# Scores and exponentials of an attention step divided by columns of four PSUM banks instead of by banks

## The chip, the core and the metric

The kernel runs on one core of one Trainium2 chip. The metric is the device time of one execution in microseconds (us), the median of several runs. A profile is one execution recorded by the hardware profiler; its own time is given beside its span, because durations are read from that one execution.

Engines are called as the profile calls them: PE is TensorE (matmuls), PEld its weight loads, ACT is ScalarE, DVE is VectorE, POOL is GpSimd, SP is SyncE[...]. PSUM is the memory that PE writes its results to. The kernel divides it into eight banks of 512 fp32 values per partition.

## What is computed

`x` is (16, 128, 512), the context `c` is (16, 128, 128), all fp32. First comes cross attention with 32 query heads and 8 key/value heads of size 16, then a mixture of 32 experts; both are added to `x`. Cut to what matters:

```python
def _L0_xattn_ref(q, k, v):                       # k = v = ctx
    qh = q.reshape(B, S, KV, G, D).transpose(0, 2, 3, 1, 4)      # 8 KV heads x 4
    kh = k.reshape(B, S, KV, D).transpose(0, 2, 1, 3)
    vh = v.reshape(B, S, KV, D).transpose(0, 2, 1, 3)
    scores = jnp.einsum('bkgsd,bktd->bkgst', qh, kh) / scale     # scale = sqrt(16)
    weights = jax.nn.softmax(scores, axis=-1)
    out = jnp.einsum('bkgst,bktd->bkgsd', weights, vh)
    return out.transpose(0, 3, 1, 2, 4).reshape(B, S, E)
...
x = x + _L0_xattn_ref(_layernorm(x, axis=-1), ctx_512, ctx_512)
x = x + _L0_ffn_ref(_layernorm(x, axis=-1), ...)                 # router, 8 of 32 experts, shared expert
```

## The kernel before

The program has two stages. `attention_small` (L301) does the attention of all 16 batches and, woven into it, the second layer norm, the turned rows for the experts and the router's logits. `experts` follows: ranking of the tokens, the shared expert, and the routed experts. A general version of the attention (`rest`, behind a flag) is taken only if some keys are long; it is not run with these inputs.

The attention is a list of 32 steps, `items = [(b, i)]`: batch `b`, and `i` the parity of the KV head. A step handles four KV heads, `j` = 0 to 3, with their four query heads each and 128 tokens, so 512 columns per KV head.

- `scores(b, i)` (L484) issues four matmuls (L489), one per `j`. Each contracts 32 rows: the stationary operand is a 32 x 128 piece of the keys `kz` (in which `odd` has zeroed the head of the other parity), the moving operand 32 rows x 512 columns of the turned queries `qT`. `tile_position=(j * HP, 0)` puts each into its own row group of PE, so the four can run beside each other. Each result, 128 keys x 512, fills one PSUM bank. Two banks make one tile of the pool `ps_sc`, which has two such tiles, tag `sc`. In the profile every fp32 matmul stands as two records, so a step has eight.
- Two exponentials follow on ACT (L499), each over one tile of two banks, 128 x 1024, into a tile of the SBUF pool `pp` (five of them).
- `values(b, i)` (L502) multiplies the exponentials with the values `va` (four matmuls, L505, 512 columns each, weights of 32 columns, one column group per `j`), and DVE copies the result (L514). A column of ones in `va` gives the sums of the exponentials along.
- `transposes(...)` (L447) turns up to two sets into one PSUM tile of the pool `ps_x` (L459): queries of a batch to come (`queries`, copied out by ACT at L480), normalized rows for the router (`turn_of`, ACT, L543), and the output of `values` (`added`, divided and added by DVE and POOL, L523 to L532).

The order of the instructions on PE, ACT, DVE and POOL is written out by hand; each engine works its queue in that order. In the loop over `n` (L650), PE gets per step: scores of step n, values of step n-1, in some steps the gate's matmuls (`gate_parts`, L566, and `gate_sums`, L581), then the transposes: one set in step 1 and in the odd steps up to 11 (none in step 0), two sets in most others. `head`, `middle` and `tail` hang further work of DVE, POOL and ACT on the steps; what of it is ACT's: `keys` (L373, ahead of the scores of steps 4, 5, 9, 11, 17 and 19) and `squares` (L394, steps 21, 23, 25 and 27). Waits between engines are put in by the framework from the tiles that instructions read and write.

Behind the last step the two tiles of `ps_sc` are used again: `two` (L685) for transposes, and `gu` (L686), two banks, for the first matmuls of the shared expert (`filler`, L282).

Of the kernel before, what the change touches and what calls it, by code (L numbers as in the profile page):

```python
# [9 lines left out]
F32 = mybir.dt.float32  # L10
F16 = mybir.dt.float16
I32 = mybir.dt.int32
AF = mybir.ActivationFunctionType
ALU = mybir.AluOpType
AX = mybir.AxisListType
PSUM = bass.MemoryType.PSUM
DRAM = bass.MemoryType.DRAM

P = 128
EPS = 1e-5  # L20
HD = 16
# [25 lines left out]
def tile_xattn_moe(  # L47
# [15 lines left out]
    nc = tc.nc  # L63
    B, S, D = x.shape
    E, _, ND, I = w1.shape
# [4 lines left out]
    TB = 512  # L70
# [93 lines left out]
    rows = dram.tile([NT * P, D + E], F32, name="rows")  # L164
# [66 lines left out]
    def gate_rows(b, eng):  # L231
        xn = xnp.tile([P, D], F32, tag="xn2", name="xn2", bufs=4)
        normalized(xn, xs[b], b, SECOND, eng)
        nc.sync.dma_start(rows[ts(b, P), 0:D], xn)
        xn2[b] = xn
# [61 lines left out]
    HP = 2 * HD  # L297
    NJ = KV // 2
    quarter = [slice(4 * k, 4 * k + 4) for k in range(NTB)]

    def attention_small():  # L301


        with ExitStack() as ph:
            kpool = ph.enter_context(tc.tile_pool(name="kp", bufs=1))
            ap2 = ph.enter_context(tc.tile_pool(name="ap2", bufs=2))
            pp = ph.enter_context(tc.tile_pool(name="pp", bufs=5))
            ps_sc = ph.enter_context(tc.tile_pool(name="ps_sc", bufs=2, space=PSUM))
            ps_x = ph.enter_context(tc.tile_pool(name="ps_x", bufs=1, space=PSUM))
            ps_lg = ph.enter_context(tc.tile_pool(name="ps_lg", bufs=1, space=PSUM))  # L310
            ps_oT = ph.enter_context(tc.tile_pool(name="ps_oT", bufs=1, space=PSUM))
            qTs, ps, oTs, xqs = {}, {}, {}, {}
            cn = kpool.tile([P, B, KV * HD], F32, name="cn")
            cTs = kpool.tile([P, B, P], F32, name="cTs")

# [53 lines left out]
            kzs = [kpool.tile([P, 4, 2, P], F32, name=f"kz{k}") for k in range(2)]  # L369
# [69 lines left out]
            H = P // 2  # L439
            halves = [slice(h * H, (h + 1) * H) for h in range(2)]  # L440

            def bank_pair(pool):
                return pool.tile(
                    [P, 2, 2, 2, P], F32, tag=("x" if pool is ps_x else "sc"), name="x"
                )

            def transposes(*sets, x=None, between=()):  # L447

                x = bank_pair(ps_x) if x is None else x
                for s, (of, split, _) in enumerate(sets):  # L450
                    for k in range(4):
                        for h, rows in enumerate(halves):
                            if split:
                                to = x[:, h, :, s, ts(k, P // 4)]
                                by = ident[rows, rows].rearrange("p (a b) -> p a b", a=2)
                            else:
                                to = x[:, h, k // 2, s, ts(k % 2, H)]
                                by = ident[rows, rows]
                            nc.tensor.matmul(  # L459
                                to,  # L460
                                lhsT=of[rows, k, :],
                                rhs=by,
                                start=True,
                                stop=True,
                                is_transpose=True,
                                tile_position=(h * H, 0),
                            )
                for s, (_, _, then) in enumerate(sets):
                    if s == len(sets) - 1:
                        for f, a in between:  # L470
                            f(*a)
                    then(x[:, :, :, s])
# [9 lines left out]
                return xn, False, then  # L482

            def scores(b, i):  # L484
                scs = [ps_sc.tile([P, 2, TB], F32, tag="sc", name="sc") for _ in range(NJ // 2)]
                qT = qTs[b].rearrange("p h r s -> p (h r s)")
                for j in range(NJ):
                    rows = slice(j * HP, (j + 1) * HP)
                    nc.tensor.matmul(  # L489
                        scs[j // 2][:, j % 2],  # L490
                        lhsT=kzs[b // 4 % 2][rows, b % 4, i, :],
                        rhs=qT[rows],
                        start=True,
                        stop=True,
                        tile_position=(j * HP, 0),
                    )
                for j, sc in enumerate(scs):
                    p = pp.tile([P, 2, TB], F32, tag="p", name="p")
                    nc.scalar.activation(p, sc, AF.Exp, scale=1.0 / HD**0.5)  # L499
                    ps[b, i, 2 * j], ps[b, i, 2 * j + 1] = p[:, 0], p[:, 1]  # L500

            def values(b, i):  # L502
                oT = ps_oT.tile([P, TB], F32, tag="oT", name="oT")
# [37 lines left out]
            def turn_of(b, copy=nc.scalar.copy):  # L541
                def then(x):
                    copy(  # L543
                        xnT[b // 4][:, :, ts(b % 4, P)].rearrange(
                            "p (r k) (h s) -> p h r k s", r=2, h=2
                        ),
                        x.rearrange("p h r (k s) -> p h r k s", k=2),
                    )

                return xn2.pop(b).rearrange("p (k d) -> p k d", d=P), False, then  # L550
# [95 lines left out]
            parts[31] = 8  # L646

            transposes(queries(0))
            keep_warm(FILL[-1])
            for n in range(N):  # L650
                for f, a in head.get(n, ()):
                    f(*a)

                scores(*items[n])
                if n == 1:
                    transposes(queries(1))
                if n > 0:
                    values(*items[n - 1])
                if n in parts and n < N - 1:
                    gate_parts(parts[n])  # L660
                sets = []
                if n % 2 == 0 and 0 < n // 2 < B - 1:
                    sets.append(queries(n // 2 + 1))
                if n in turned:
                    sets.append(turn_of(turned[n]))
                if n > 1:
                    sets.append(added(*items[n - 2], nc.gpsimd if n < N - 1 else nc.vector))
                if n == N - 1:
                    sets.reverse()
                between = middle.get(n, ())  # L670
                if sets:
                    transposes(*sets, between=between)
                else:
                    assert not between
                keep_warm(FILL.get(n, 0))
                if n in sums:
                    gate_sums(sums[n])
                for f, a in tail.get(n, ()):
                    f(*a)
# [2 lines left out]

            gate_rows(12, nc.gpsimd)
            nc.scalar.activation(table, table, AF.Sigmoid)
            two = bank_pair(ps_sc)  # L685
            gu = ps_sc.tile([P, 2, TB], F32, tag="sc", name="gu")  # L686
            banks = iter([gu[:, i] for i in range(2)])
            later, products = [], []
            matmuls = shared_up(0, 0, lambda: next(banks), later, products)

# [20 lines left out]
            filler(1)  # L711
            gate_parts(12)
            gate_rows(15, nc.vector)
            transposes(turn_of(15), x=bank_pair(ps_sc))
            gate_rows(14, nc.vector)
            transposes(turn_of(14, nc.vector.tensor_copy))
            gate_sums(12, nc.scalar.copy)
# [1199 lines left out]

    pieces = [(k, i) for k in range(NTB) for i in range(NI)]
    left_over = attention_small()
    experts(pieces[1:], in_order, *left_over)  # L1920
    left = nc.values_load(
# [64 lines left out]
```

## Time and profile before

| what | value |
|---|---|
| median of 3 runs | 876.24 us (875.76 to 877.6) |
| profiled execution: its time / its span | 875.97 us / 874.1 us |
| granted PE clock, mean | 0.997 |
| exponentials L499, ACT, 128 x 1024 | 64, 62.1 us busy, mean 1023 ns |
| score matmuls L489, PE, 512 columns | 256 records, 44.2 us busy |
| value matmuls L505, PE, 512 columns | 256 records, median 605 ns |
| ACT waiting for scores (L499 <- PE sc L489) | 13.2 us in 22 waits |
| score weight loads waiting for exponentials (PEld sc L489 <- ACT p L499) | 4.7 us in 13 waits, within 8.80 to 106.00 |
| scores of step 0 start / last step's start | 8.83 / 102.76 us |
| last matmul of the program ends | 864.66 us |

Times inside the profile are counted from the span's start. "Busy" is the union of an engine's instruction records; matmuls overlap in it, so a row group's matmuls that run beside each other count once. A name such as `p<-sc` is the tile written and the tile read. A releaser behind an arrow (`<-ACT p`) is what an engine's idle time ended with. The chain of waits is the sequence of pieces, each released by the one before it, that leads to the end of the span or of a window; its shares say which work the time went through.

### The profile page before, as it was taken

The page shows a single profiled execution, that of the slowest core. Times are in us where ns is not written, and L with a number is a line of the kernel's source. Part 1 is how long each engine was busy: PE and PEld are TensorE (multiplying, and loading weights), DVE is VectorE, ACT ScalarE, POOL GpSimd, SP SyncE. Part 2 cuts the span into 40 slices and gives each one's busy share as a digit, 9 for nine tenths or more (in the row PEclk, how much of TensorE's full clock was granted, in tenths as well). Part 3 has the DMA queues.
Part 4 walks back from the last instruction along what each step waited for, and adds up shares of the span by engine and source line. Part 5 has one row for each costly group of instructions (what it writes and reads, how often), then busy time and mean ns, then how long its engine had stood idle before and what let it go on. Part 6 is the DMA issues. An engine that isn't in the chain of part 4 may idle for free.

```text
span 874.1 us, 13629 instructions
## 1 busy us (share of the span) xinstructions
PE 860.4 (98%) x4015; PEld 539.0 (62%) x4015; DVE 625.7 (72%) x1599; ACT 689.3 (79%) x1570; POOL 478.7 (55%) x590
## 2 busy tenths in 40 slices
PE   8999999999999999999999999999999999999995
PEld 5344444545665666666666666676667777777763
DVE  7877778859877777777777777786777677777410
ACT  5889732539998898879898989898798889899721
POOL 4487560044355666566556665655555555664554
PEclk9999999999999999999999999999999999999998
DMA  9111112657567787788778777877787677776654
GB/s 301 66 49 40 60 50 70 218 152 206 154 176 158 171 192 200 165 174 192 159 178 195 204 171 186 197 199 177 169 180 183 166 168 195 180 188 166 94 79 53
DMA packets 59877, 137.15 MB, mean 157 GB/s; under 512 B 12169, under 2 KB 16393, under 8 KB 59793
## 3 DMA queue, kind: packets, MB, share of 16 engines
q0 software_dynamic: 32032, 69.25, 41.0%
q1 hardware_dynamic: 27680, 66.81, 22.8%
q8 instruction: 34, 0.56, 0.3%
q14 instruction: 51, 0.41, 0.2%
q10 hardware_dynamic: 80, 0.13, 0.1%
HBM read 96.71 MB, written 46.73 MB: 164 GB/s over the span
## 4 chain that ended last, share of the span: by engine, by line
PE 92%; POOL 3%; issue 2%; DMA 2%; ACT 1%; DVE 0%; POOLq 0%; ACTq 0%
PE p L1611 43%; PE y L1749 24%; PE gu L282 6%; PE sc L489 5%; PE oT L505 4%; PE y L1386 3%; PE x L459 2%; POOL out_dram L1721 2%; DMA out_dram<-yw,token 2%; PE gu L1541 2%; PE tok L1038 1%; PE lgT L566 0%; PE lg L581 0%; ACT p L499 0%; PE rank L1277 0%
## 5 line engine op out<-in xcount | busy, mean ns | idle before, releaser
L1506 ACT COPY xall<-blocks 32x256 f32<-32x256 f32 (+10 forms) x1137 | 419.1, 369 | 15.0
L1721 POOL DMA_INDIRECT out_dram<-yw,token x150 | 243.6, 1624 | 210.7 <-DMA out_dram<-yw,token 78.6
L1749 PE MATMUL y<-wdn,sa 128*128 128x512 f32 (+2 forms) x672 | 259.1, 594 | 0.0
L1460 POOL DMA_INDIRECT xgs<-rows,token x138 | 155.4, 1126 | 128.1 <-DVE token L1050 53.2
L1611 PE MATMUL p<-xall,wup 128*128 128x270 f32 (+27 forms) x720 | 185.4, 394 | 0.0
L1611 PEld LDWEIGHTS p<-xall,wup 128*128 128x128 f32 x720 | 136.7, 190 | 44.1 <-issue 16.9
L1749 PEld LDWEIGHTS y<-wdn,sa 128*128 128x128 f32 (+2 forms) x672 | 100.9, 171 | 83.7 <-issue 70.5
L1765 ACT ACTIVATE yw<-y,wt 128x512 f32<-128x512 f32 x138 | 94.7, 686 | 71.0 <-PE y L1749 39.0
L1611 PE MATMUL p<-t,s 128*128 128x270 f32 (+27 forms) x480 | 125.6, 394 | 0.0
L1611 PEld LDWEIGHTS p<-t,s 128*128 128x128 f32 x480 | 91.1, 190 | 37.6 <-issue 22.4
L1509 DVE STREAM_TRANSPOSE blocks<-xgs 128x512 f32<-128x512 f32 x138 | 97.3, 705 | 0.2
L1621 DVE TENSOR_TENSOR z<-u,p 128x270 f32<-128x270 f32 (+27 forms) x96 | 48.8, 508 | 66.9 <-PE p L1611 63.2
L499 ACT ACTIVATE p<-sc 128x1024 f32<-128x1024 f32 x64 | 62.1, 1023 | 13.3 <-PE sc L489 13.2
L1611 PE MATMUL p<-t,wup 128*128 128x270 f32 (+27 forms) x240 | 63.7, 396 | 0.0
L1611 PE MATMUL p<-xall,s 128*128 128x270 f32 (+27 forms) x240 | 63.5, 395 | 0.0
L1611 PEld LDWEIGHTS p<-t,wup 128*128 128x128 f32 x240 | 45.1, 190 | 24.8 <-issue 14.1
L282 PE MATMUL gu<-xall,sup 128*128 128x512 f32 x128 | 59.2, 602 | 0.0
L1621 DVE TENSOR_TENSOR u<-u,p 128x270 f32<-128x270 f32 (+27 forms) x48 | 24.4, 508 | 44.2 <-PE p L1611 37.1
L1611 PEld LDWEIGHTS p<-xall,s 128*128 128x128 f32 x240 | 45.3, 190 | 15.9 <-issue 3.9
L1506 DVE COPY xall<-blocks 32x256 f32<-32x256 f32 (+11 forms) x187 | 50.7, 298 | 3.5
L489 PE MATMUL sc<-qT,kz 32*128 32x512 f32 x256 | 44.2, 639 | 0.5 <-ACT p L499 0.2
L1602 DVE TENSOR_TENSOR t<-xall,t 128x540 f32<-128x540 f32 (+27 forms) x60 | 43.4, 723 | 0.5
(218 smaller groups left out, 916.0 us busy)
## 6 DMA issues: line engine op xcount, KB each, us to landing
wup<-in_w_dram SPq DMA_DIRECT2D x64, 512.0 KB, 4.8
wdn<-in_w_dram SPq DMA_DIRECT2D x32, 512.0 KB, 5.9
rows<-xn SPq DMA_DIRECT2D x16, 256.0 KB, 2.0
out_dram<-x SPq DMA_DIRECT2D x16, 256.0 KB, 3.3
x<-in_x_dram SPq DMA_DIRECT2D x15, 256.0 KB, 5.3
out_dram<-yw,token POOLq DMA_INDIRECT x150
xgs<-rows,token POOLq DMA_INDIRECT x138
cTs<-in_cT_dram SPq DMA_DIRECT2D x4, 256.0 KB, 4.7
```

The source lines that it names most:

```text
L282: nc.tensor.matmul(acc, lhsT=sup[:, w, d, ts(i, P)], rhs=xnT[k][:, d, :], start=(d == 0), stop=(d == ND - 1),)
L489: nc.tensor.matmul(scs[j // 2][:, j % 2], lhsT=kzs[b // 4 % 2][rows, b % 4, i, :], rhs=qT[rows], start=True, stop=True, tile_position=(j * ...
L499: nc.scalar.activation(p, sc, AF.Exp, scale=1.0 / HD**0.5)
L1460: nc.gpsimd.indirect_dma_start(out=t, out_offset=None, in_=rows[:, :], in_offset=bass.IndirectOffsetOnAxis(ap=token[:, j : j + 1], axis=0) ...
L1506: yield on_ACT, 1 + many, lambda dst=dst, of=of, copy=copy: copy(dst, of)
L1509: nc.vector.transpose(blocks[:, j % NB_BUF, :], xgs[:, j % NG_BUF, 0:D])
L1602: yield lambda o=out_, a=a, b=b: nc.vector.tensor_tensor(o, a, b, ALU.subtract)
L1611: nc.tensor.matmul(acc[:, i, 0:h], lhsT=w[:, i, d, :], rhs=x[:, d, :], start=(first and i == d == 0), stop=(i == outs[-1] and d == 1), ski ...
L1621: soon(lambda: nc.vector.tensor_tensor(out_, a, b, ALU.add))
L1721: ins = nc.gpsimd.indirect_dma_start(out=flat, out_offset=bass.IndirectOffsetOnAxis(ap=token2[:, k - 1 : k] if a else token[0:b, j : j + 1 ...
L1749: nc.tensor.matmul(y[c0:c1, :], lhsT=acts_of[k % NA][:, i, col : col + c1 - c0], rhs=wdn[k % NW][:, i, :], start=(i == 0), stop=(i == NI - 1),
L1765: nc.scalar.activation(yws[j], y, AF.Copy, scale=wt[:, j : j + 1])
```

## The change

`ps_sc` now holds one tile `sc` for the whole attention, `[P, NJ, 2, TB // 2]`: four banks (index `j`), each split into two halves of 256 columns (index `h`). A step issues, for `h` = 0 and then 1, four matmuls of 256 columns, one into each bank, followed by one exponential over that half of all four banks (128 x 4 x 256, the same 1024 columns). There are eight score matmuls a step in place of four, with half the columns; the number of exponentials and their size stay. The exponentials of a step go to one tile `p` of four times 512 columns; `pp` has three such tiles (before, five tiles of half the size). `values` reads the same columns as before. The scratch `two` is now banks 0 and 1 of `sc`, the banks of `gu` are its banks 2 and 3.

```diff
-            pp = ph.enter_context(tc.tile_pool(name="pp", bufs=5))
-            ps_sc = ph.enter_context(tc.tile_pool(name="ps_sc", bufs=2, space=PSUM))
+            pp = ph.enter_context(tc.tile_pool(name="pp", bufs=3))
+            ps_sc = ph.enter_context(tc.tile_pool(name="ps_sc", bufs=1, space=PSUM))
...
+            sc = ps_sc.tile([P, NJ, 2, TB // 2], F32, name="sc")
...
             def scores(b, i):
-                scs = [ps_sc.tile([P, 2, TB], F32, tag="sc", name="sc") for _ in range(NJ // 2)]
-                qT = qTs[b].rearrange("p h r s -> p (h r s)")
+                p = pp.tile([P, NJ, 2, TB // 2], F32, tag="p", name="p")
+                qT = qTs[b].rearrange("p h r s -> p h (r s)")
+                for h in range(2):
+                    for j in range(NJ):
+                        rows = slice(j * HP, (j + 1) * HP)
+                        nc.tensor.matmul(
+                            sc[:, j, h],
+                            lhsT=kzs[b // 4 % 2][rows, b % 4, i, :],
+                            rhs=qT[rows, h],
+                            start=True,
+                            stop=True,
+                            tile_position=(j * HP, 0),
+                        )
+                    nc.scalar.activation(p[:, :, h], sc[:, :, h], AF.Exp, scale=1.0 / HD**0.5)
                 for j in range(NJ):
-                    rows = slice(j * HP, (j + 1) * HP)
-                    nc.tensor.matmul(
-                        scs[j // 2][:, j % 2],
-                        lhsT=kzs[b // 4 % 2][rows, b % 4, i, :],
-                        rhs=qT[rows],
-                        start=True,
-                        stop=True,
-                        tile_position=(j * HP, 0),
-                    )
-                for j, sc in enumerate(scs):
-                    p = pp.tile([P, 2, TB], F32, tag="p", name="p")
-                    nc.scalar.activation(p, sc, AF.Exp, scale=1.0 / HD**0.5)
-                    ps[b, i, 2 * j], ps[b, i, 2 * j + 1] = p[:, 0], p[:, 1]
+                    ps[b, i, j] = p[:, j].rearrange("p h t -> p (h t)")
...
-            two = bank_pair(ps_sc)
-            gu = ps_sc.tile([P, 2, TB], F32, tag="sc", name="gu")
-            banks = iter([gu[:, i] for i in range(2)])
+            two = sc[:, 0:2].rearrange("p h r (s t) -> p h r s t", s=2)
+            banks = iter([sc[:, i].rearrange("p h t -> p (h t)") for i in (2, 3)])
...
-            transposes(turn_of(15), x=bank_pair(ps_sc))
+            transposes(turn_of(15), x=two)
```

The helper `bank_pair` is gone; `transposes` takes its tile from `ps_x` itself when it is given none.

## The prediction, made before the changed kernel ran

> **What bounds the kernel now.** I read the page's first rows, then the table by windows, to see which engine fills the attention stage, 8.80 to 106.00 us, and what follows it.
>
> ```profile
> PE 860.4 (98%) x4015; PEld 539.0 (62%) x4015; DVE 625.7 (72%) x1599; ACT 689.3 (79%) x1570; POOL 478.7 (55%) x590
> ```
>
> ```profile
> 8.80:106.00 97.20, 96.77 (x1008) 39.75 (x1009) 76.49 (x187) 81.59 (x103) 57.66 (x115) 1.00 0.27 93
> 106.00:146.00 40.00, 38.46 (x228) 18.46 (x228) 30.48 (x117) 10.80 (x21) 15.91 (x154) 1.00 0.09 34
> 146.00:868.00 722.00, 718.66 (x2740) 474.60 (x2738) 513.54 (x1278) 594.10 (x1442) 398.97 (x288) 1.00 0.73 173
> ```
>
> The columns after the window's length are busy PE, PEld, DVE, ACT and POOL. TensorE (PE) is the bound everywhere: behind the attention it stands idle 1.5 us of 40 and 3.3 us of 722, so time lost in the attention goes into the end time almost whole. Within the attention, PE's 96.77 us is not all streaming, so I read the chain of waits of that window: its line shares, then one pair of steps.
>
> ```profile
> by line: PE sc L489 43.4%; PE oT L505 30.7%; PE x L459 19.1%; PE lg L581 2.3%; ACT p L499 2.1%; PE lgT L566 1.8%; PE gu L282 0.6%; issue 0.3%; PE kT L411 0.2%
> ...
> 40.98 1.07 PE sc L489 x8
> 42.05 1.00 PE oT L505 x8
> 43.05 0.39 PE x L459 x8
> 43.44 1.82 PE sc L489 x8
> 45.26 1.00 PE oT L505 x8
> 46.26 0.64 PE x L459 x16
> ```
>
> A step is scores, values of the step before, transposes. The scores take 1.07 when nothing stops them and up to 1.82 when their second pair of banks is still being read by the last step's second exponential. In all they hold 43.4% of 97.2 = 42.2 us, 1.32 a step; without any wait 32 x 1.07 = 34.2. So about 8 us of the stage is waiting for ScalarE: all that a better overlap could win. The timeline of ScalarE and PE shows the couplings that I need.
>
> ```profile
> 42.15 1.94 ACT L499 ACTIVATE p<-sc 128x1024 f32<-128x1024 f32 x2
> 44.60 1.94 ACT L499 ACTIVATE p<-sc 128x1024 f32<-128x1024 f32 x2 [0.52 <-PE sc L489]
> ...
> 48.07 1.94 ACT L499 ACTIVATE p<-sc 128x1024 f32<-128x1024 f32 x2 [0.54 <-PE sc L489]
> ```
>
> ```profile
> 43.37 1.90 PE L489 MATMUL sc<-qT,kz 32*128 32x512 f32 x8
> ...
> 46.83 1.14 PE L489 MATMUL sc<-qT,kz 32*128 32x512 f32 x8
> ```
>
> Unhindered scores start at 46.83, the last ends 1.14 later (47.97), and the exponentials start at 48.07: 0.10 from PE to ScalarE. In the step at 43.37 the second pair ends at 45.27, so it began at 44.13, 0.04 to 0.05 after the exponential that ended at 44.09: that is the release back to PE. One exponential takes 1.02 (the page: x64, mean 1023 ns).
>
> **The change, part by part.** *The waits.* The first group of four matmuls now fills columns 0 to 255 of all four banks, the first exponential reads those, the second group fills the other halves. [...] Row first: in the step at 43.37 the second pair streams from 44.13 to 45.27 while the first exponential reads from 44.60 on; they are in different banks. [...] By columns, as the change has it, the second group could stream under the first exponential[...]. No trace of before has two engines in one bank, but the order of the built program decides it: the second group of each step waits for that step's first exponential, and the first group of the next step for the second exponential. (The transposes of the odd steps have lost their own wait for ScalarE, as the new one covers it.) So scores and exponentials of a step run one after the other: group, exponential, group, exponential. Behind the waiting second group PE's queue holds the values of the step before and the transposes, which have nothing to do with that exponential.
>
> *The group.* Four matmuls of 512 columns take 1.07 to the next start. Half is 0.54. The row nearest to four matmuls of 256 columns is the gate's.
>
> ```profile
> 82.93 0.61 PE L566 MATMUL lgT<-xall,gw 128*32 128x256 f32 x8
> ```
>
> It loads 32 weight columns, not 128 (weight loads: 110 ns against 182). [...] The eight records of a group are two passes over the same row groups[...]. The rows alone, 0.61 with its tail, put it at 0.55 to 0.62; I take 0.64, as it explains the 0.08 that score passes are longer than value passes (records start 0.53 against 0.45 apart). The last result comes 0.07 after the next start (1.14 - 1.07), so a group is complete at 0.71.
>
> *The exponential.* Same 1024 columns, now four runs of 256, strided on both sides. The query copy reads runs of 128 (512 in 586 ns), the gate copy a plain run (256 in 378): 0.81 ns a column, as the exponential has from 512 to 1024 ((1023 - 586)/512 = 0.85). Runs cost nothing that shows; bounds 0 and 5% (+3 us in all), I take 0.
>
> *One step.* Scores start at 0; complete 0.71; exponential from 0.81 to 1.83; second group from 1.88; values at 1.88 + 0.64 = 2.52, where before it was 1.32. The second exponential ends at 1.88 + 0.71 + 0.10 + 1.02 = 3.71, and PE comes to the next scores at 2.52 + 1.00 + 0.39 = 3.91 at the earliest (one set of transposes) or 4.16 (two): the wait across steps is gone, by 0.15 to 0.4. Sum for steps 1 to 31: 31 x 2.52 = 78.1, against 42.2 - 1.1 (step 0) = 41.1: **+37.0**.
>
> *Step 0.* Its first exponential starts at 10.00 as before (ScalarE copies values until then), ends 11.02; second group 11.07; second exponential 11.88 to 12.90; step 1 starts at 12.95, before at 11.07: **+1.9**.
>
> *ScalarE's queue.* The first exponential is now waited for by PE at once, so what ScalarE does before it counts.
>
> ```profile
> 23.26 0.58 ACT L480 COPY qT<-x 128x512 f32<-128x512 f32 x1
> 23.74 0.73 ACT L373 ACTIVATE kz<-cTs,odd 128x512 f32<-128x512 f32 x1
> 24.39 1.94 ACT L499 ACTIVATE p<-sc 128x1024 f32<-128x1024 f32 x2
> ```
>
> That step's scores start at 23.15, so copy and keys hold the exponential until 1.24 after the start in place of 0.81. A copy alone ends in time (0.11 + 0.49 = 0.60). Keys come behind a copy in steps 5, 9, 11, 17 and 19: 5 x 0.43 = 2.1; squares in steps 21, 23, 25, 27 (85.29 - 84.12 = 1.17): 4 x 0.36 = 1.4. **+3.5**, 1.5 to 5.5. Two small waits of PE for ScalarE outside the scores (steps 4 and 9) go: **-0.3**.
>
> *At nothing:* fewer, larger `p` buffers (3 steps in place of 2.5), since values follow one step behind; VectorE and GpSimd, whose work stays the same and had 20 and 40 us to spare; the two score pairs used as scratch behind step 31, where the order is the same and the banks are free by then (3.71 against 4.16). If work behind the attention had waited for something else than PE, it could give back at most the 1.5 us idle there; I take 0.
>
> Sum: 37.0 + 1.9 + 3.5 - 0.3 = +42.1. The profiled execution took 875.97 (span 874.1 and 1.9 around it), so 918.1; it lies 0.27 below the median of 876.24, which gives **918.3**.
>
> **Rivals.** *Faster: the columns do run free.* If the second group streams under the first exponential, PE pays 2 x 0.64 = 1.28 a step and waits for nothing, as the exponential starts 0.4 earlier: 31 x 1.28 = 39.7 against 41.1, 874.8; with a hidden reload 31 x 1.07, 868.3. It decides from the point where the second group's wait is met before PE gets there; ScalarE's 2.4 a step would fit under PE's 2.7. Middle 872. For it: 8 us of waits are there to win. Against it: the wait in the built program[...]. 2%.
>
> *Much slower: the clock falls.* PE now stands 1.25 of some 4 us in every step. If that takes the granted clock to half, 2.9 us of streaming a step double: +90, 1008. Against it, the windows behind the last matmul (864.66):
>
> ```profile
> 864.70:868.50 3.80, 0.00 (x0) 0.00 (x0) 0.00 (x0) 0.69 (x1) 2.57 (x2) 1.00 0.81 115
> 868.60:872.00 3.40, 0.00 (x0) 0.00 (x0) 0.00 (x0) 0.00 (x0) 0.00 (x0) 0.50 0.04 9
> ```
>
> The clock held 1.00 for 3.8 us without a matmul; the new gaps are a third of that. 3%.
>
> **How the numbers follow.** The serial case has 95%. Its low end: groups at the gate's row (0.10 sooner and 0.09 shorter: -5.9), queue -2, 1.5 given back: 909. Its high end: exponential +3, queue +2, both weight loads dearer (182 - 110 ns each, +0.05 twice a step: +3): 927. The rivals' 5% stay outside the range. A change within 0.2% is about what measurement cannot tell here; nothing lands there but the dearest form of the first rival: faster 2%, same 1%, slower 97%.
>
> **What would show it.** In the profile after: the score line at some 80 us of the attention's chain together with exponentials, PE idle some 1.2 us in nearly every step "<-ACT p" ahead of the second four matmuls, no two exponentials back to back (they stand in pairs of 1.94 now), 32 steps in about 139 us, granted clock 1.00, and everything behind shifted unchanged. It is wrong if exponentials overlap the second group's records, if score groups take 0.54, or if the stage behind takes more or less than its 762 us.

## The result, and the profile after

The changed kernel takes 925.0 us, the median of six runs (920.72 to 930.74). The kernel before takes 876.04 us in its six runs beside it (875.76 to 877.6). The ratio is 1.056, interval 1.052 to 1.060: slower, by 49 us. The forecast was 918.3, with a range of 909 to 927.

The profiled execution is the slowest of the six, 930.74 us (span 928.9). Its page, first the engines' row and the clock's, then the two costly groups that the change touches:

```profile
PE 873.0 (94%) x4271; PEld 548.3 (59%) x4271; DVE 626.3 (67%) x1599; ACT 694.5 (75%) x1570; POOL 479.4 (52%) x590
...
PEclk7989999999999999999999999999999999999998
...
L495 ACT ACTIVATE p<-sc 128x1024 f32<-128x1024 f32 x64 | 65.5, 1023 | 45.3 <-PE sc L487 44.0
...
L487 PE MATMUL sc<-qT,kz 32*128 32x256 f32 x512 | 49.7, 460 | 42.0 <-ACT p L495 41.7
```

ScalarE has the same 64 exponentials at the same mean of 1023 ns, but now stands idle 44.0 us for score matmuls (13.2 before); PE stands idle 41.7 us for exponentials (0.2 in the same row before). Each engine waits for the other. And a row that was expected to stay as it was did not: the mean granted clock is 0.982, and the dip is in the first slices, where the attention is.

The table by windows, cut at the same points of the program as before (attention; 40 us behind it; the routed experts):

```profile
8.80:159.80 151.00, 109.15 (x1263) 49.06 (x1263) 76.65 (x187) 86.53 (x103) 57.76 (x119) 0.91 0.18 62
159.80:199.80 40.00, 38.14 (x232) 18.45 (x229) 29.69 (x116) 10.81 (x21) 15.30 (x150) 1.00 0.09 31
199.80:921.80 722.00, 719.35 (x2741) 474.86 (x2739) 514.79 (x1279) 594.34 (x1442) 400.21 (x288) 1.00 0.74 173
```

All of it is in the first window: from the first score to the first matmul of the shared expert it is 150.9 us, before 96.9. From there to the last matmul it is 759.3 us, before 758.9. DVE and ACT have the same number of instructions in the attention as before (187 and 103; POOL has 119 in this window and had 115); PE has 255 records more, at a granted clock of 0.91.

The chain of waits over the attention, by lines, and a step on PE and on ScalarE from the timeline (start, length, engine, line, and in brackets the idle time before it with what ended it):

```profile
by line: PE sc L487 27.5%; PE oT L502 23.8%; ACT p L495 21.6%; PE x L456 13.3%; issue 4.5%; DMA cn<-in_c_dram 4.0%; ACT qT L477 2.4%; PE lg L578 1.5%; ACT sq L395 1.3%; PE lgT L563 1.1%; PE warm L354 1.0%; ACT kz L374 0.6%; ACT va L383 0.4%
```

```profile
41.44 0.71 PE L487 MATMUL sc<-qT,kz 32*128 32x256 f32 x8
43.36 0.71 PE L487 MATMUL sc<-qT,kz 32*128 32x256 f32 x8 [1.20 <-ACT p L495]
44.00 1.06 PE L502 MATMUL oT<-p,va 128*32 128x512 f32 x8
```

```profile
42.28 1.02 ACT L495 ACTIVATE p<-sc 128x1024 f32<-128x1024 f32 x1
44.14 1.02 ACT L495 ACTIVATE p<-sc 128x1024 f32<-128x1024 f32 x1 [0.83 <-PE sc L487]
```

First group 41.44, complete 42.15; exponential 42.28 to 43.30; second group 43.36; values 44.00. The exponentials stood in pairs before; now each has a group of matmuls ahead of it and, for the first, one behind it that waits. From scores to values it is 2.56 us at full clock, where before it was 1.32 on average. The exponential, 2.1% of the chain before, is 21.6% of it.

The clock in two windows in a row (length, then busy time and instructions of PE, PEld, DVE, ACT and POOL, then the granted clock):

```profile
48.88:52.29 3.41, 1.84 (x36) 1.20 (x32) 3.06 (x7) 2.36 (x4) 0.49 (x1) 1.00 0.02 5
52.29:55.71 3.42, 3.42 (x28) 1.22 (x24) 1.24 (x4) 1.02 (x1) 0.23 (x1) 0.50 0.00 0
```

PE worked 1.84 of 3.41 us at the full clock; the next 3.41 us were granted half of it. The changes of the clock in this trace lie 3.41 us or a multiple of it apart (11.33, 21.57, 52.29, 55.71). Eight windows of 3.41 us at half clock, 27.3 us, lie in the attention of this execution, three of them before 21.6 us. The steps in them are longer than other steps of their kind by 10.9 us in all (0.25 to 2.1 each). The other five executions show mean clocks of 0.986 to 0.996 and are shorter in that order.

### The profile page after: what moved, and what is told of

The parts are those of the page before. It is cut to its first block, busy times and chain, and to the rows that moved or that the text cites. A ratio compares the mean times of both kernels' runs of the same rounds, so it can differ in the third digit from the quotient of the medians.

```text
span 928.9 us, 14113 instructions
## 1 busy us (share of the span) xinstructions
PE 873.0 (94%) x4271; PEld 548.3 (59%) x4271; DVE 626.3 (67%) x1599; ACT 694.5 (75%) x1570; POOL 479.4 (52%) x590
## 4 chain that ended last, share of the span: by engine, by line
PE 87%; ACT 5%; issue 3%; POOL 2%; DMA 2%; SPq 0%; DVE 0%; POOLq 0%; ACTq 0%; DVEq 0%
PE p L1607 41%; PE y L1745 23%; PE gu L282 5%; PE sc L487 4%; PE oT L502 4%; ACT p L495 4%; PE y L1382 3%; PE x L456 2%; POOL out_dram L1717 2%; PE gu L1537 1%; DMA out_dram<-yw,token 1%; PE tok L1034 1%; PE sc L282 1%; DMA cn<-in_c_dram 1%; PE lg L578 0%
## 5 line engine op out<-in xcount | busy, mean ns | idle before, releaser
L495 ACT ACTIVATE p<-sc 128x1024 f32<-128x1024 f32 x64 | 65.5, 1023 | 45.3 <-PE sc L487 44.0
L487 PE MATMUL sc<-qT,kz 32*128 32x256 f32 x512 | 49.7, 460 | 42.0 <-ACT p L495 41.7
L511 DVE COPY oTs<-oT 128x512 f32<-128x512 f32 x32 | 22.1, 691 | 60.0 <-PE oT L502 60.0
L529 POOL TENSOR_TENSOR x<-x,at 128x256 f32<-128x256 f32 x30 | 21.8, 725 | 72.2 <-DVE at L522 72.2
L487 PEld LDWEIGHTS sc<-qT,kz 32*128 32x128 f32 x512 | 21.7, 198 | 60.1 <-ACT p L495 55.7
```

The source lines that it names most:

```text
L487: nc.tensor.matmul(sc[:, j, h], lhsT=kzs[b // 4 % 2][rows, b % 4, i, :], rhs=qT[rows, h], start=True, stop=True, tile_position=(j * HP, 0),)
L495: nc.scalar.activation(p[:, :, h], sc[:, :, h], AF.Exp, scale=1.0 / HD**0.5)
```

## The experiments

My theory when they began had four parts. (A) PE and ScalarE work in turns because the second group waits for the first exponential, and PE's queue blocks what stands behind it; this is worth some +43. (B) The wait comes from the shared banks. (C) Part of the time is the second load of the same weights. (D) On top, the clock falls where PE stands idle. The rival to B is that the wait comes with the one lasting tile, whatever the banks; the rival to C, that the load is hidden; the rival to D, that PE's idle time drops the clock by its length alone. Kernel before beside them: 875.9 on each chip.

| label | change | median (range), us | ratio, interval |
|---|---|---|---|
| e1 | one lasting tile, divided by banks | 883.75 (883.69 to 884.01) | 1.0087, 1.0072 to 1.0101 |
| e2 | by columns, both exponentials after all matmuls | 883.97 (883.82 to 885.48) | 1.0094, 1.0079 to 1.0109 |
| e3 | the change, gap filled with full matmuls | 922.07 (920.85 to 922.34) | 1.0521, 1.0507 to 1.0534 |
| e4 | the change, gap filled with thin matmuls | 926.5 (922.81 to 927.33) | 1.0568, 1.0549 to 1.0586 |
| e5 | before, with split score matmuls | 876.15 (875.97 to 878.15) | 1.0005, 0.9997 to 1.0013 |
| e6 | the change, values moved into the gap | 903.36 (902.02 to 903.61) | 1.0303, 1.0287 to 1.0319 |
| e9 | e3, without filling in five steps | 922.35 (922.13 to 923.47) | 1.0529, 1.0514 to 1.0543 |

One further run of e4, 947.61 at a mean clock of 0.963, is left out of its row; no trace of it was kept. Three more kernels (e7, e8, e10) compute half of the heads and are read in their attention alone: their attention values differ, a general part (`rest`) ran behind, and so their totals, about 3.6 ms, say nothing.

**e1: the lasting tile without the columns.** Four matmuls of 512 columns into the four banks of the one tile, then an exponential on banks 0 and 1 and one on banks 2 and 3, as the kernel before has it with two tiles.

```diff
-                for h in range(2):
-                    for j in range(NJ):
...
-                            sc[:, j, h],
...
+                for j in range(NJ):
...
+                        sc[:, j].rearrange("p h t -> p (h t)"),
...
+                for k in (slice(0, 2), slice(2, 4)):
+                    nc.scalar.activation(p[:, k], sc[:, k], AF.Exp, scale=1.0 / HD**0.5)
```

> One lasting tile of four banks and three large p buffers, but scores and exponentials divided by banks as before. Theory 'by tile' (a score matmul waits for every earlier exponential on its tile, whichever banks that reads): the scores of a step wait for the second exponential of the step before, so a step lasts at least 1.14 + 0.12 + 1.94 + 0.05 = 3.25 us where it was 2.71 or 3.2 in turns: 29 steps, 94.3 against 88.3, about 882. Theory 'by bank' (only a shared bank makes it wait): the tile changes nothing, 876.

It measured 883.75, 7.9 above before. Its timeline, first the exponentials of one step on ScalarE, then the scores of the next two steps on PE:

```profile
35.89 1.94 ACT L495 ACTIVATE p<-sc 128x1024 f32<-128x1024 f32 x2 [1.32 <-PE sc L486]
```

```profile
37.88 1.14 PE L486 MATMUL sc<-qT,kz 32*128 32x512 f32 x8 [0.48 <-ACT p L495]
...
41.14 1.14 PE L486 MATMUL sc<-qT,kz 32*128 32x512 f32 x8 [0.73 <-ACT p L495]
```

All four matmuls start together at 37.88, when the second exponential of the step before has ended (35.89 + 1.94 = 37.83). The one into bank 0 has no bank in common with that exponential, which reads banks 2 and 3, and it waits all the same. So the wait comes with the tile, and B is refuted. This part of the change alone makes a step as long as its scores and both exponentials one after the other: 3.26 here, 3.03 on average before (96.9 / 32).

**e2: the columns without the turns.** The change, with the exponentials moved behind all eight matmuls.

```diff
                             tile_position=(j * HP, 0),
                         )
+                for h in range(2):
                     nc.scalar.activation(p[:, :, h], sc[:, :, h], AF.Exp, scale=1.0 / HD**0.5)
```

> All eight score matmuls of a step first, then the two exponentials, still by columns. The wait inside the step is gone, the wait across steps and the second weight load stay. Serial theory: a step lasts 1.28 + 0.07 + 0.12 + 1.94 + 0.05 = 3.46, about 889.5; the wait inside a step is then worth some 30 of the 44 us. If the loss were in the 256-column matmuls or in the strided exponentials, it would stay at 915 to 920. PE is used more, so the clock should hold 1.00.

It measured 883.97, the same as e1, 5.5 under the expectation, at mean clocks of 0.996 and 0.997 (0.995 to 0.998 before). On PE:

```profile
37.90 1.15 PE L487 MATMUL sc<-qT,kz 32*128 32x256 f32 x16 [0.48 <-ACT p L496]
38.98 1.06 PE L503 MATMUL oT<-p,va 128*32 128x512 f32 x8
```

Eight matmuls of 256 columns hold PE for 1.08, as long as four of 512 (1.07). Loading the weights twice costs nothing, which speaks against C. Dividing by columns is harmless in itself: it is free in PE and, as the exponential keeps its 1.02 with four runs of 256, free in ScalarE. What costs is the order, an exponential between the groups of one tile: from 884.0 to 919.3, the change's time at full clock (derived under e3 and e9).

**e5: the reload alone.** The kernel before, each score matmul of 512 columns issued as two of 256, pair of banks by pair of banks.

```diff
-                for j in range(NJ):
+                for k, h, j in [(k, h, 2 * k + d) for k in range(2) for h in range(2) for d in range(2)]:
...
-                        scs[j // 2][:, j % 2],
+                        scs[k][:, j % 2, cols],
```

> The kernel before, each score matmul of 512 columns issued as two of 256 (tiles, banks and exponentials as before). If the weight load of 128 columns is paid again per group[...], scores take 1.28 in place of 1.07 where nothing stops them, less where they wait for an exponential: 879 to 882. If it hides: 876.

```profile
46.99 1.16 PE L490 MATMUL sc<-qT,kz 32*128 32x256 f32 x16
```

It measured 876.15, a ratio that is no different from 1, with scores 1.09 long where they were 1.07: C is refuted. The single records, whose starts I take from the trace of e2, show how. Its four rounds of records (one record per row group in each; in the trace of before, the four of a round start within 0.02 and last 0.69 or 0.59 each) start at 0, 0.321, 0.537 and 0.753, and the values at 1.075. Rounds in the middle are 0.216 apart, each with a load of 128 weight columns of its own. Where matmuls of the routed experts follow in a row in the trace of before, they start 0.216 apart with 256 columns (L1541) and 0.429 with twice as many (L1749): the columns account for all of it, and no load shows. Some 0.105 more is seen twice. In the first round (0.321 = 0.105 + 0.216) it fits a load that nothing covers: in the trace of before the two loads of a row group start 0.108 apart there (46.83 and 46.94). In the hand-over to the values (0.322) it does not fit one: the values load 32 columns, and their own first round, 0.453 in place of 0.429, is only 0.024 longer for it. What fills the hand-over stays open. In the kernel before it is the same: 0, 0.535 and 1.070, with 0.429 for 512 columns. Both ends are paid once per block. The second group of the changed kernel is a block by itself: its second round starts 0.320 after its first (43.36 and 43.68), and the values 0.324 after that (44.00), 0.64 in all.

**e6: other work into the gap.** The values of the step before, which need neither exponential of this step, are issued between the two groups.

```diff
-                scores(*items[n])
+                scores(*items[n], (lambda: values(*items[n - 1])) if n > 0 else None)
...
-                if n > 0:
-                    values(*items[n - 1])
```

> The changed kernel with the values of the step before issued between the two score groups. Serial theory: PE's work now fits under the exponentials, and the chain group, exponential, group, exponential sets the step: 2 x (0.71 + 0.12 + 1.02 + 0.05) = 3.8 us, about 904, with the clock at 1.00 or nearly. If PE's own time set the step, it would change nothing: 920 to 930.

It measured 903.36, as expected. On PE, a step's second group (its transposes, left out, follow), then the next step's first group, the values that were moved, and its second group:

```profile
41.13 0.71 PE L489 MATMUL sc<-qT,kz 32*128 32x256 f32 x8 [0.21 <-ACT p L497]
...
42.99 0.71 PE L489 MATMUL sc<-qT,kz 32*128 32x256 f32 x8 [0.50 <-ACT p L497]
43.63 1.07 PE L504 MATMUL oT<-p,va 128*32 128x512 f32 x8
45.00 0.71 PE L489 MATMUL sc<-qT,kz 32*128 32x256 f32 x8 [0.30 <-ACT p L497]
```

From group to group it is 1.86 and 2.01, and each waits for an exponential: groups and exponentials in turns are now the whole step (3.87 here; 3.95 or 4.20 in the changed kernel at full clock), and values and transposes lie beside them. The clock held 1.00 in the attention, but behind it one window fell to half:

```profile
143.01:146.42 3.41, 2.55 (x33) 1.91 (x34) 0.69 (x1) 1.52 (x5) 0.00 (x0) 1.00 0.00 0
146.42:149.83 3.41, 3.41 (x5) 1.35 (x5) 2.44 (x8) 2.08 (x3) 3.29 (x7) 0.50 0.01 2
```

In this execution (903.61) the part behind the attention takes 761.0 us, against 759.3 in the other changed forms, so at full clock e6 is some 901.9. Of the 43 us that the change costs at full clock, the work blocked behind the waiting group is then 919.3 - 901.9 = 17; the turns themselves are the other 26.

**e7, e8, e10: tile or bank, in the changed order.** With two KV heads in place of four, each half of the columns can have banks to itself. e7 keeps the change's layout, both halves in the same two banks of the tile; e10 puts the second half into two other banks of the same tile; e8 gives it a tile of its own.

```diff
-                    for j in range(NJ):
+                    for j in range(2):
...
e7    sc[:, j, h]              exponential from sc[:, 0:2, h]
e10   sc[:, 2 * h + j, 0]      exponential from sc[:, 2 * h : 2 * h + 2, 0]
e8    scs[h][:, j, 0]          exponential from scs[h][:, :, 0]
```

> The changed kernel with two KV heads per step in place of four in scores and exponentials (values use their weights twice, the other heads' scores are left out), both halves of the columns in the same two banks. Second group starts 0.71 + 0.12 + 0.59 + 0.05 = 1.47 after the first, values at 2.11; about 903 at full clock, more by what the clock loses, as the array is used less.

> The same with half the heads left out, but the second half of the columns in two other banks, in a tile of its own. The second group needs no exponential of its step: it starts 0.64 after the first, values at 1.28, about 874; against the one with shared banks some 28 us less for the same work. If the reload and the smaller matmuls were the cost, both would take the same.

> Half the heads left out as before; the second half of the columns goes to two other banks, but of the same tile. If the wait comes with the tile, the second group starts 1.45 after the first, as with shared banks; if it comes with the bank, 0.5 to 0.64 after it, as with two tiles.

The timelines on PE, first e7, then e10, then e8:

```profile
44.22 0.70 PE L487 MATMUL sc<-qT,kz 32*128 32x256 f32 x4
45.68 0.70 PE L487 MATMUL sc<-qT,kz 32*128 32x256 f32 x4 [0.76 <-ACT p L495]
```

```profile
43.22 0.70 PE L487 MATMUL sc<-qT,kz 32*128 32x256 f32 x4
44.68 0.70 PE L487 MATMUL sc<-qT,kz 32*128 32x256 f32 x4 [0.76 <-ACT p L495]
```

```profile
42.16 1.13 PE L487 MATMUL sc<-qT,kz 32*128 32x256 f32 x8
43.22 1.07 PE L502 MATMUL oT<-p,va 128*32 128x512 f32 x8
```

The second group starts 1.46 after the first whether it shares banks with the exponential or not; with a tile of its own it follows at once, and values start after 1.06 in place of 2.09 (1.28 was expected, with the reload that e5 rules out). That is the rival to B again, now in the order that costs the time. The clock of e7 fell as well: it was 0.50 from 50.90 to 54.31, and 0.976 to 0.983 in the mean of its four runs. A version of the whole step with a tile for each half and, as in all kernels here, a bank for each score matmul of a half needs all eight banks into which the kernel divides PSUM for its scores, and the transposes, the gate and the values hold four. It was not built, nor was a layout with two heads in one bank; no kernel here beats the one before.

**e3, e4: the clock.** Idle matmuls on zeros are put into the gap ahead of the second group, whose results nobody reads: three of 128 x 128 x 128 (e3), or four of 32 x 32 x 128 (e4). They are meant to fill PE's time about alike (in e3 the three take 0.94 at 42.10) and to differ in how much of the array they use. In both kernels the tile of the idle matmuls is taken anew at each use, from the pool that the gate uses too.

```diff
                 for h in range(2):
+                    if h == 1:
+                        keep_warm(3)       # e4: four matmuls idle[0:32] <- wz[0:32, 0:32], wz[0:32]
                     for j in range(NJ):
```

> The changed kernel with three idle matmuls of 128 x 128 x 128 on zeros in PE's gap between the two score groups; they end before the exponential does. Clock theory (the granted clock falls when the array's use in a window of 3.41 us is below some 0.37): no half-clock window in the attention, all runs within 919 to 922. Rival (the spread of 921 to 931 comes from something else, as from the DMAs): time and spread as in the changed kernel.

> As the run with full idle matmuls, but each fills 32 rows x 32 columns of the array only: the gap is busy, the array's use hardly rises (some 0.015). If use counts, the clock still falls in some windows and runs lie at 921 to 931; if the length of the gap or PE's busy time counts, no window falls and all runs are within 919 to 922.

The attention of e3 by windows, then two windows in a row of e4:

```profile
8.70:150.30 141.60, 125.49 (x1455) 68.95 (x1455) 76.67 (x187) 86.41 (x103) 58.68 (x124) 1.00 0.19 66
```

```profile
141.54:144.96 3.42, 3.06 (x44) 2.27 (x40) 2.38 (x6) 1.61 (x2) 0.72 (x1) 1.00 0.16 62
144.96:148.37 3.41, 3.41 (x33) 1.14 (x25) 0.69 (x1) 1.02 (x1) 0.00 (x0) 0.50 0.23 82
```

In the profiled run of e3 the clock stays at 1.00, and it takes 920.85, ten less than the profiled run of the change with the same serial steps; its runs spread over 1.5 us and not 10. The cure is not whole: three of the five runs, 922.07 to 922.34 and so at or just over the expected end, show a mean clock of 0.994 to 0.995 in place of 0.997. That would fit one more window at half clock; they have no trace. About 1.55 us of the 920.85 are waits that the idle matmuls add (their bank is also the gate's, and in step 31 they wait 1.3 for its reader), so the change at full clock is some 919.3. In e4 a window in which PE is 89% busy is followed by half the clock, so the thin matmuls did not hold it up; the runs of e4 lie where they were expected if use counts. D stands in the form that use decides; its rival, the length of idle time, is refuted.

To see what does count I took every window of 3.41 us in the attention of ten profiles (before, after, e1 to e8), and added up for each matmul its rows x columns of the array x columns streamed, as a share of 128 x 128 at 1.2 columns per ns (512 columns took 0.429 us above, 1.19 per ns).

| window granted | next one | windows | share of the array used | PE busy |
|---|---|---|---|---|
| full clock | half | 15 | 0.14 to 0.379 | 0.44 to 0.89 |
| full clock | full | 307 | 0.353 and up, nearly all over 0.383 | 0.54 and up |
| half clock | half | 35 | up to 0.378 | 0.67 to 1.00 |
| half clock | full | 14 | 0.386 and up | 0.94 and up |

Use of about 0.38 parts them in both directions, with an overlap of three windows; busy time does not separate them. The attentions of e9 and e10, which were not used to find the boundary, agree: six windows of 0.25 to 0.34 were followed by half the clock, six at half clock with 0.389 and more by the full one, and those that stayed at half have 0.372 at most, though two that stayed at full clock have only 0.366 and 0.369. The kernel before ran its attention at 0.55 and more. The longest gap in the windows of the changed kernel that fell was 1.7 us. What exactly the chip counts stays open: the share is a quantity that parts these windows, and of its factors only the size of the idle matmuls was varied on purpose.

**e9: fill only where it seems needed.** e3 without idle matmuls in steps 18, 22, 26, 30 and 31, to save the waits that they add there.

```diff
-                    if h == 1:
+                    if h == 1 and 2 * b + i not in (18, 22, 26, 30, 31):
```

> As the run with full idle matmuls, but without them in steps 18, 22, 26, 30 and 31, where they waited for a reader of the gate's bank and held the step up by 3.3 us in all. If serial waits and the clock are all there is, this is the changed kernel at full clock: 918 to 919, up to 1.5 more where one of the five bare steps falls into a window of low use. The prediction's sum without a clock term was 918.3.

A miss: 922.35, no better than e3. In its profile two windows with half the clock came back (106.94 to 110.35 and 144.48 to 147.90), behind windows with bare steps. The first of them, with the one ahead of it:

```profile
103.53:106.94 3.41, 2.21 (x32) 1.36 (x32) 1.70 (x5) 1.61 (x2) 1.39 (x5) 1.00 0.00 0
106.94:110.35 3.41, 3.41 (x32) 1.48 (x28) 1.15 (x2) 1.60 (x3) 2.63 (x10) 0.50 0.00 0
```

The steps in them are 2.7 longer. Step 0 is another 0.44 longer than in e3, as the context lands later there (ScalarE starts to copy it at 9.82 in place of 9.36). The profiled run took 922.49; 922.49 - 2.7 - 0.44 = 919.35, the same full-clock time as from e3.

## Why the prediction was right, and where its reasons were not

**The serial step: right.** 2.52 was forecast from scores to values, 2.56 measured; over 31 steps that is 1.2 more than the sum had. At full clock the change costs 919.3 - 875.9 = 43.4, against a sum of 42.1.

**ScalarE's queue: right, a little smaller.** Steps with keys behind a copy are +0.37 (0.43 forecast), steps with squares +0.27 (0.36): 5 x 0.37 + 4 x 0.27 = 2.9 in place of 3.5. Step 14 is +0.32, which the forecast did not have; its cause stays open.

**At nothing: right.** Exponentials over runs of 256 keep 1023 ns; what lies behind the attention is 0.4 longer; the wait across steps is gone in most steps, as the step is now longer than that wait.

**Why the second group waits: the wait was read rightly from the built program, its reason wrongly.** I put it down to the banks that the second group shares with the exponential: an assumption, which no trace of before shows. What two engines in one bank at once would do, no kernel here shows either. The wait is the framework's, for the tile: e1 and e10 have it with separate banks, e8 is free of it with separate tiles. It made no difference to the time, but it would have to the cure: other banks of the same tile do not help.

**The group of 0.64: right number, wrong working.** It was my estimate, and that a load is paid in each of a group's two passes was not shown by any trace of before. With 0.108 for a load of 128 columns, as the loads at 46.83 and 46.94 stand apart, it is (1.07 - 2 x 0.108)/2 + 2 x 0.108 = 0.64. e5 and e2 refute the working for these matmuls: the same reload inside a running block costs nothing (ratio 1.0005). Of the two loads that the estimate counted, one is real, at the start of a block (0.321 in place of 0.216 in e2); the other 0.105 stands at the hand-over to the values, where no load of that size is due. With two passes in a group both accounts give 0.64, which is luck. With four they part, and there the wrong one made the expectation for e2 5.5 too high.

**The clock: the step that failed.** It was a rival at 3%, written as all or nothing: +90 if the clock falls, nothing otherwise, and dismissed because it had held 1.00 for 3.8 us without a matmul. That view does not show how much idle time a window of 3.41 us may hold. The clock fell in part, in 8 windows of the profiled execution. The windows of 3.41 us do not keep step with the kernel's 3.95 or 4.20, so it is likely that in each execution others of them hold too little work; the other five runs have a mean clock and no trace. Against 919.3 the fastest run is 1.4 us longer, the profiled one 11.4 (10.9 read from its steps, the other 0.5 at its two ends), the median 5.7. These 5.7 are what is left over, not a measurement of their own, and the clock is their only cause that the traces show: 875.9 + 43.4 + 5.7 = 925.0. The range of 909 to 927 held the median without a term for this cause, so that part of the hit is luck; two of the six runs, 927.79 and 930.74, lie beyond its end. The length of a gap was the wrong measure: the clock held 1.00 for 3.8 us without a matmul in before (864.70 to 868.50), and fell here with gaps of at most 1.7, behind windows in which 0.379 of the array or less was used.

**What would have shown it.** The signs named in the prediction came: no pairs of exponentials, PE idle 1.20 "<-ACT p" ahead of the second four matmuls (41.7 in all, 1.3 a step), everything behind merely shifted. The 139 us named for the 32 steps is 150.9 less 10.9 for the clock, 140.0. "Granted clock 1.00" was the sign that failed.

## What to carry to other kernels

Before dividing work inside one tile, ask what the automatic waits are keyed on: here it is the tile, so two halves that should overlap need two tiles (the second group follows at once in e8); other columns or banks of one tile are not enough (1.46 after the first in e7 and e10). A wait put in the middle of an in-order queue costs its own length and blocks everything behind it; if it must be there, put work that does not depend on it into the gap (17 us of 43 here). And when PE, full before (96.8 us of 97.2), begins to stand idle (151.0 - 109.2 = 41.8 of 151.0 us here), price the clock too: here the share of the array used per window told which windows fell (at 0.379 and less), and the length of a gap (at most 1.7 us) did not.

## What the hardware showed that was not expected

In these traces the granted clock follows how much of the array is used in windows of 3.41 us, with a boundary near 0.38 both for falling (15 windows, at 0.14 to 0.379) and for recovering (14, at 0.386 and up). PE busy for 89% of a window with small matmuls (use 0.325) lost the clock, and 100% busy at half clock with a use up to 0.378 did not win it back. Three idle 128 x 128 x 128 matmuls per step, some 0.9 us of PE, took the spread between runs from 10 us to 1.5. One half-clock window behind the attention made the profiled run of e6 1.7 us longer.

A weight load into a row group in which a matmul is streaming is hidden here: 256-column passes follow at 0.216 us in e2 with a new load of 128 columns for each, and only the first load of a block, 0.105, is seen. As much again passes at the hand-over to the values (0.322 in place of 0.216), and its cause is open.
